# Block transposes of the mirrored squares one item behind their scores, and more room between the steps of the next batch's group norm

## The chip, the cores and the metric

The kernel runs on one core of one Trainium2 chip. The metric is device time in microseconds of one execution, the median over the runs shown; lower is better. The engines are TensorE (PE in the profile, with its weight loads as PEld), VectorE (DVE), ScalarE (ACT), GpSimd (POOL) and SyncE (SP), which only issues transfers here.

## The reference

The input x is float32 of shape (8, 128, 48, 48): 8 batches, 128 channels, 2304 positions. With C = 128 and n, m over positions:

```
# layer 0, for each batch
g   = group_norm(x, 32 groups)
x0  = concat(g, position embedding of 32 channels)
q,k,v = leaky_relu(W x0 + b)                    # each 128 x 2304
A   = softmax(q^T k / sqrt(128), masked to m <= n)
x   = x + v A^T                                 # causal attention
# layer 1, tokens t = x^T, 2304 x 128 a batch
h   = layer_norm(t)
t   = t + softmax(h h^T) h                      # full attention, no mask
u   = layer_norm(t) W^T, batch-normalized over all 8 x 2304 rows
y_s = sigmoid(u_s + y_{s-1} V^T)                # a recurrence over positions
out = t + y
```

Two facts of layer 1 matter. The score matrix h h^T is symmetric, so a block of exponentials (i, j) is the transpose of the block (j, i). And the group norm of batch b+1 depends on x alone, so it can be done while batch b is still in its attention.

## The kernel before

**Tiles.** Everything is float32. The 2304 positions of a batch are 18 blocks of 128 (NB), in 6 chunks of 384 columns (NQ = 6, QC = 384, QB = 3 blocks a chunk). One chunk of output stands in one PSUM bank and is summed over the 18 blocks of the other side.

**Two attentions as one stream of items.** For each batch, an object of `Causal` and one of `Full` list their items (method `items`). An item is one block m against one chunk j. `begin` issues its scores: a matmul into PSUM (line 1313 in `Full`), then ScalarE's exponential into a tile `p` in SBUF (line 1315). `product` issues the second matmul, which adds the item to the chunk's output `o` (line 1335), and does so three items later (LAG = 3 in the main loop, line 1518). A chunk's last product is followed by `after`, which copies `o` out and adds a chain of steps for the residual and the norm behind it. Batches follow each other in the one stream, so the next batch's projections and first scores mix with the end of the batch before.

**The symmetry in `Full`.** Chunk j computes scores only for blocks m >= 3j. There are three kinds of items:

- *direct*: scores and exponentials as above. Within the chunk's own 3 x 3 square of blocks, only the upper part is computed: own block g covers the columns from g x 128 on, so its matmuls have 384, 256 and 128 columns (`offset`). Own blocks 0 and 1 are begun first in a chunk.
- *turned*: for m < 3j the block was computed in chunk i < j, and is used transposed. VectorE transposes 32 x 32 squares when it was direct (`turned`, line 1280), SP stores the result as `e` (line 1229), and loads it back later as `g` (line 1221). Its product is line 1323.
- *mirrored*: the lower part of the chunk's own square, at the chunk's end (line 1331). It comes from `mirror`: two transposes on VectorE, `tm<-p` (line 1248), of 256 columns for own block 0 and 128 for own block 1. After the second, two transfers on GpSimd's queue follow: `m<-tm` (`out_of`, line 1261, to DRAM) and `gm<-m` (`back_in`, line 1265, four issues). The first must have landed before the second is issued. `mirror` is called from `product`, so three items behind the scores.

**Who decides the order.** The kernel writes its own order: within `manual_schedule` each engine executes instructions in the order in which Python emits them. Matmuls of the items form the backbone. Everything else (projections of the next batch, group norm, residuals, transfers) is a `Chain` of steps, and `Stream` keeps an account of time with which it places them: `now` is TensorE's, and `free` has one entry each for VectorE, ScalarE and GpSimd. A step is a triple: the work, its TensorE cost, and a list of (engine, us) that follows it. `Stream.then` books these on the engine's account, in turn; an entry with an empty name adds time without an engine, for a transfer or for room. A chain's next step is due at the time that `then` returns, and `tick`, called after each item, runs up to two steps that are due. So a number in such a list moves no work by itself: it moves the item after which the next step is emitted, and a booking made earlier also moves the due times of other chains.

**The group norm of the next batch.** `group_norm(b + 1)` is added as a chain when chunk 1 of `Full(b)` begins. `part1` has six `bn_stats` of 384 columns on VectorE and an aggregate (lines 805 and 807). `part2` averages over the groups with a tiny matmul, `gn_m` (line 813), and finishes with three small VectorE instructions. `part3` has a second tiny matmul, `gn_v` (line 824), one VectorE addition and the inverse square root on GpSimd (`gn_rs`, line 669). Its result is first read when the projection of the next batch starts, in chunk 4 (`begin`, j == NQ - 2).

**The residual behind a chunk of `Full`.** TensorE turns the output back (`of_t`, line 957), VectorE does the division, the residual, three pairs of statistics and a transpose (`dn` at line 1370 to `tt` at 1386), GpSimd a root (`roots`, line 1392), VectorE a small transpose of it (line 1397). SP stores root and row (`spread`, lines 1403 and 1406), loads them in another layout (`fetch`, lines 1410 and 1412), and TensorE multiplies by the weight (`wx`, line 1418), scaled on VectorE (1419) and copied by ScalarE (1424).

After the last batch, the recurrence runs over all batches at once (line 1660).

Of the kernel before, what the change touches and what calls it, by code (L numbers as in the profile page):

```python
# [604 lines left out]
def fast_path(ctx: ExitStack, tc: tile.TileContext, x, pe, w_ffn, out, x_tok, w_qkv, w_pos, v_t, gamma_beta, flag):  # L605
# [7 lines left out]
    QC = 384  # L613
    NQ = N // QC
    QB = QC // P
    SCALE = 1.0 / math.sqrt(P)
    US = 4 / 2400.0
# [46 lines left out]
    def rsqrt(pool, out_ap, var_ap, eps, tag):  # L664

        n = out_ap.shape[-1]
        ve = pool.tile([P, n], F32, tag=f"ve_{tag}", name=f"ve_{tag}")
        nc.vector.tensor_scalar_add(ve, var_ap, eps)
        nc.gpsimd.tensor_tensor(out_ap, ve, mhalf[:, :n], ALU.pow)

    with ExitStack() as actx:
# [16 lines left out]
        def psum_s(name):  # L688
            return ps_s.tile([P, CH], F32, tag="s", name=name)

        def psum_t(name):
            return ps_t.tile([P, CH], F32, tag="t", name=name)
# [97 lines left out]
        st = Stream()  # L790
# [7 lines left out]
        def group_norm(b):  # L798
            xt = xbuf[b]
            c = {}  # L800

            def part1():
                gs = small2.tile([P, NQ, 6], F32, tag="gn_st", name=f"gn_st_{b}")
                for j in range(NQ):
                    nc.vector.bn_stats(gs[:, j, :], xt[:, ts(j, QC)])  # L805
                mv = small2.tile([P, 2], F32, tag="gn_mv", name=f"gn_mv_{b}")
                nc.vector.bn_aggr(mv, gs)
                c["mv"] = mv

            def part2():  # L810
                mv = c["mv"]
                tp = psum_t(f"gn_m_{b}")
                nc.tensor.matmul(tp[:, 0:1], grp, mv[:, 0:1], start=True, stop=True)
                mg = small2.tile([P, 1], F32, tag="gn_mg", name=f"gn_mg_{b}")
                nc.vector.tensor_copy(mg, tp[:, 0:1])
                d = small.tile([P, 1], F32, tag="gn_d", name=f"gn_d_{b}")
                nc.vector.tensor_sub(d, mv[:, 0:1], mg)
                e = small2.tile([P, 1], F32, tag="gn_e", name=f"gn_e_{b}")
                nc.vector.scalar_tensor_tensor(e, d, d, mv[:, 1:2], ALU.mult, ALU.add)
                c["mg"], c["e"] = mg, e  # L820

            def part3():
                tp = psum_t(f"gn_v_{b}")
                nc.tensor.matmul(tp[:, 0:1], grp, c["e"], start=True, stop=True)
                rs = small2.tile([P, 1], F32, tag="gn_rs", name=f"gn_rs_{b}")
                rsqrt(small2, rs, tp[:, 0:1], 1e-5, "gn")
                norm_of[b] = c["mg"], rs

            return [(part1, 0.0, [("DVE", 3.6)]), (part2, 0.15, [("DVE", 0.6)]), (part3, 0.15, [("DVE", 0.15), ("POOL", 0.9)])]


        keys, vals, queries, largest, projected = {}, {}, {}, {}, {}
# [174 lines left out]
        class Causal:  # L1007


            def __init__(self, b):  # L1010
                self.b, self.sums, self.whose = b, {}, {}
# [14 lines left out]
            def begin(self, j, m, first):  # L1026
                b = self.b
                if first and b and j == 0:
                    st.advance(moved[b - 1], 2)
                if first:  # L1030
                    st.finish(projected[b, j])
                    allowed[b] = j + EARLY
                    following(b)
                    if j == NQ - 1:
                        bounds(b)
                off = self.offset(j, m)
                s = psum_s(f"s_{b}_{j}_{m}")
                nc.tensor.matmul(s[:, off:QC], keys[b][:, ts(m, P)], queries[b, j][:, off:], start=True, stop=True)  # L1038
                p = pp.tile([P, QC], F32, tag="p", name=f"p_{b}_{j}_{m}")
                nc.scalar.activation(p[:, off:], s[:, off:QC], AF.Exp, scale=SCALE)  # L1040
                ops = [("ACT", 0.16 + (QC - off) * 0.00085)]
                if m >= QB * j:
                    nc.gpsimd.tensor_mul(p[:, off : off + P], p[:, off : off + P], triu)  # L1043
                    ops.append(("POOL", 0.5))
                return p, st.then(st.spend((QC - off) * US), ops)
# [139 lines left out]
        class Full:  # L1185
# [6 lines left out]
            def __init__(self, b):  # L1192
                self.b = b
                self.tiles, self.stored, self.loaded = {}, {}, {}
                self.pairs = [(i, j) for j in range(NQ) for i in range(j)]
                self.used, self.to_store = 0, deque()

            @staticmethod
            def items():
# [88 lines left out]
            def begin(self, j, what, first):  # L1288
                b = self.b
                if j == 0:  # L1290
                    st.finish(normed_chunks[b, min(what[1] + 1, NB - 1) // QB])
                if first and b + 1 < B:
                    if j == 1:
                        norm_chain[b + 1] = st.add(group_norm(b + 1))
                    if j == NQ - 2:
                        st.finish(norm_chain[b + 1])
                        project(b + 1, 0)
                self.prefetch()
                if what[0] == "turned":
                    i, g = what[1:]  # L1300
                    while (i, j) not in self.loaded:
                        while self.pairs[len(self.loaded)] not in self.stored:
                            self.store()
                        self.load()
                    return self.loaded[i, j][:, :, g, :, :].rearrange("p a m r -> p m a r"), 0.0
                if what[0] == "mirrored":
                    st.finish(moved[b])
                    return self.gm.rearrange("p a q r -> p q a r"), 0.0
                m = what[1]
                off = self.offset(j, m)  # L1310
                xh = x_hat[b][1]
                s = psum_s(f"s1_{b}_{j}_{m}")
                nc.tensor.matmul(s[:, off:QC], xh[:, ts(m, P)], xh[:, j * QC + off : (j + 1) * QC], start=True, stop=True)  # L1313
                p = pp.tile([P, QC], F32, tag="p", name=f"p1_{b}_{j}_{m}")
                nc.scalar.activation(p[:, off:], s[:, off:QC], AF.Exp, bias=shift)  # L1315
                return p, st.then(st.spend((QC - off) * US), [("ACT", 0.17 + (QC - off) * 0.00085)])

            def product(self, j, what, o, p, ready, first, last):
                xhT = x_hat[self.b][0]
                if what[0] == "turned":  # L1320
                    i, g = what[1:]
                    out_ap = o[:, :QC].rearrange("p (m a r) -> p m a r", m=QB, a=R)
                    nc.tensor.matmul(out_ap, xhT[:, QB * i + g, :], p, start=first, stop=last)  # L1323
                    if g == QB - 1:
                        self.used += 1
                    cols = QC
                elif what[0] == "mirrored":
                    g = what[1]
                    cols = g * P
                    out_ap = o[:, :cols].rearrange("p (m a r) -> p m a r", m=g, a=R)  # L1330
                    nc.tensor.matmul(out_ap, xhT[:, QB * j + g, :], p[:, g - 1 : 2 * g - 1], start=first, stop=last)  # L1331
                else:
                    off = self.offset(j, what[1])
                    cols = QC - off
                    nc.tensor.matmul(o[:, off:QC], xhT[:, what[1], :], p[:, off:], start=first, stop=last)  # L1335
                    g = what[1] - QB * j
                    if g >= QB:
                        self.turned(j, what[1], p, ready)
                    elif g < QB - 1:
                        self.mirror(j, g, p, ready)  # L1340
                st.spend(cols * US, ready)

# [159 lines left out]
        for j in range(3):  # L1502
            positions(0, j)
        gn = st.add(group_norm(0))
        idle(psum_s("idle_m"), 2)
        st.advance(gn, 2)
# [23 lines left out]
        ready, o = {}, {}  # L1530
        for n in range(len(stream) + LAG):
            if n < len(stream):
                part, j, what, first, last = stream[n]
# [5 lines left out]
            if n >= LAG:  # L1539
                part, j, what, first, last = stream[n - LAG]  # L1540
# [16 lines left out]
    with ExitStack() as rctx:  # L1557
# [130 lines left out]
        off = rc.tile([P, 1], F32, tag="off", name="off")  # L1688
# [60 lines left out]
```

## Time and profile before

| | us |
|---|---|
| median of 3 runs | 1727.7 (1722.65, 1727.7, 1728.26) |
| the profiled execution | 1721.34 |
| its span in the profile | 1719.6 |
| TensorE busy | 1689.9 (98%) |
| VectorE busy | 1204.8 (70%) |
| ScalarE busy | 681.0 (40%) |
| GpSimd busy | 455.0 (26%) |
| mean granted TensorE clock | 0.996 |

The span is from the first to the last instruction that the profile holds; 1.7 us of the execution lie around it. The profile comes from one execution. The page gives busy time by engine, the chain of work that ended last (followed back from the end), groups of instructions with what ended the idle time before them, and transfers. Answers from the trace add the waits of one engine (who waited for whom, in total, how often, the longest) and a timeline. In these lines `p<-s` means a tile p written from a tile s; buffer and batch numbers are left out, so `gm<-m` stands for all batches and chunks. A float32 matmul shows as two passes, so a count of x2 is one matmul.

### The profile page before, as it was taken

The page shows a single profiled execution, that of the slowest core. Times are in us where ns is not written, and L with a number is a line of the kernel's source. Part 1 is how long each engine was busy: PE and PEld are TensorE (multiplying, and loading weights), DVE is VectorE, ACT ScalarE, POOL GpSimd, SP SyncE. Part 2 cuts the span into 40 slices and gives each one's busy share as a digit, 9 for nine tenths or more (in the row PEclk, how much of TensorE's full clock was granted, in tenths as well). Part 3 has the DMA queues.
Part 4 walks back from the last instruction along what each step waited for, and adds up shares of the span by engine and source line. Part 5 has one row for each costly group of instructions (what it writes and reads, how often), then busy time and mean ns, then how long its engine had stood idle before and what let it go on. Part 6 is the DMA issues. An engine that isn't in the chain of part 4 may idle for free.

```text
span 1719.6 us, 22539 instructions
## 1 busy us (share of the span) xinstructions
PE 1689.9 (98%) x6258; PEld 1084.3 (63%) x6259; DVE 1204.8 (70%) x3297; ACT 681.0 (40%) x1300; POOL 455.0 (26%) x637
## 2 busy tenths in 40 slices
PE   9999999999999999999999999999999999999996
PEld 5666666666666666666666666666666666666675
DVE  5875578656886478855687567865688657985467
ACT  3344324442344423434244333444234442344445
POOL 1222122411233222321224212332213312232115
PEclk9999999999999999999999999999999999999998
DMA  3347864568454884368644785457844587237867
GB/s 121 90 100 210 237 184 117 125 198 249 125 127 127 246 237 127 78 175 251 195 119 93 214 234 167 120 133 215 240 133 102 149 245 239 54 82 227 224 252 223
DMA packets 316732, 291.68 MB, mean 170 GB/s; under 512 B 195793, under 2 KB 280690, under 8 KB 315956
## 3 DMA queue, kind: packets, MB, share of 16 engines
q1 hardware_dynamic: 306572, 268.76, 54.9%
q0 software_dynamic: 9792, 20.99, 4.6%
q8 instruction: 52, 0.85, 0.2%
q14 instruction: 84, 0.69, 0.1%
q10 hardware_dynamic: 232, 0.40, 0.1%
HBM read 164.13 MB, written 125.90 MB: 169 GB/s over the span
## 4 chain that ended last, share of the span: by engine, by line
PE 88%; DMA 5%; DVE 4%; issue 1%; POOL 1%; SPq 1%; ACT 0%; DVEq 0%; POOLq 0%; ACTq 0%
PE s L1038 17%; PE o L1049 17%; PE s L1313 15%; PE o L1335 14%; PE o L1323 11%; PE pj L899 3%; DMA e<-t 2%; PE o L1331 2%; PE z L1660 2%; PE wx L1418 2%; PE pj L902 1%; DMA gm<-m 1%; DMA m<-tm 1%; PE of_t L957 1%; DVE gn_st L805 1%
## 5 line engine op out<-in xcount | busy, mean ns | idle before, releaser
L1315 ACT ACTIVATE p<-s,shift 128x384 f32<-128x384 f32 (+2 forms) x504 | 274.3, 550 | 562.7 <-PE s L1313 510.3
L1040 ACT ACTIVATE p<-s 128x384 f32<-128x384 f32 (+2 forms) x504 | 230.3, 460 | 399.7 <-PE s L1038 330.2
L1038 PE MATMUL s<-q,k 128*128 128x384 f32 (+2 forms) x1008 | 380.7, 459 | 0.0
L1313 PE MATMUL s<-xh 128*128 128x384 f32 (+2 forms) x1008 | 379.0, 458 | 0.0
L1049 PE MATMUL o<-p,vT 128*128 128x384 f32 (+2 forms) x1008 | 377.7, 456 | 0.0
L1335 PE MATMUL o<-p,xhT 128*128 128x384 f32 (+2 forms) x1008 | 367.8, 456 | 0.0
L1280 DVE STREAM_TRANSPOSE t<-p 128x384 f32<-128x384 f32 x360 | 183.4, 549 | 157.4 <-DMA e<-t 93.8
L1323 PE MATMUL o<-g,xhT 128*128 128x384 f32 x720 | 280.2, 486 | 0.0
L1335 PEld LDWEIGHTS o<-p,xhT 128*128 128x128 f32 x1008 | 189.6, 190 | 120.7 <-ACT p L1315 0.9
L1049 PEld LDWEIGHTS o<-p,vT 128*128 128x128 f32 x1008 | 186.7, 190 | 109.9 <-POOL p L1043 3.1
L1313 PEld LDWEIGHTS s<-xh 128*128 128x128 f32 x1008 | 183.6, 190 | 101.1
L1038 PEld LDWEIGHTS s<-q,k 128*128 128x128 f32 x1008 | 182.8, 190 | 98.5 <-issue 2.2
L1064 DVE TENSOR_TENSOR acc<-acc,p 128x384 f32<-128x384 f32 (+2 forms) x408 | 211.1, 517 | 24.2 <-DVE acc L1064 0.5
L1323 PEld LDWEIGHTS o<-g,xhT 128*128 128x128 f32 x720 | 131.8, 190 | 75.4 <-DMA g<-e 0.5
L1043 POOL TENSOR_TENSOR p<-p,triu 128x128 f32<-128x128 f32 x144 | 72.4, 505 | 343.5 <-ACT p L1040 343.3
L1265 POOL DMA_DIRECT2D gm<-m x192 | 107.0, 562 | 90.7 <-DMA m<-tm 50.4
L1392 POOL TENSOR_TENSOR roots<-ve_f,mhalf 128x3 f32<-128x3 f32 x48 | 41.9, 873 | 241.0 <-DVE ve_f L941 240.8
L947 POOL TENSOR_TENSOR rs_c<-ve_c,mhalf 128x3 f32<-128x3 f32 x48 | 48.3, 1006 | 173.3 <-DVE ve_c L941 173.2
L1138 POOL TENSOR_SCALAR xhT<-xhT 128x384 f32<-128x384 f32 x48 | 61.8, 1287 | 74.4 <-DVE yt L1150 39.1
L899 PE MATMUL pj<-xn,wT 128*128 128x384 f32 x192 | 79.3, 496 | 1.2 <-DVE xn L892 1.2
L1261 POOL DMA_DIRECT2D m<-tm x48 | 29.0, 603 | 189.7 <-DVE tm L1248 189.3
L1419 DVE TENSOR_TENSOR scale<-wx,scale 128x384 f32<-128x384 f32 x46 | 25.6, 557 | 74.0 <-PE wx L1418 66.4
(255 smaller groups left out, 1678.7 us busy)
## 6 DMA issues: line engine op xcount, KB each, us to landing
e<-t SPq DMA_DIRECT2D x480, 144.0 KB
g<-e SPq DMA_DIRECT2D x120, 576.0 KB
pb<-posb_d SPq DMA_DIRECT2D x42, 576.0 KB
t1t<-in_x_tok_dram SPq DMA_DIRECT2D x48, 192.0 KB
m<-tm POOLq DMA_DIRECT2D x48, 192.0 KB, 5.5
gm<-m POOLq DMA_DIRECT2D x192, 48.0 KB, 3.2
t_d<-tt SPq DMA_DIRECT2D x184, 48.0 KB
t2x<-t_d SPq DMA_DIRECT2D x46, 192.0 KB
```

Source lines behind the costliest of these rows:

```text
L899: nc.tensor.matmul(ps[:, :QC], wT[:, j, :], xn, start=True, stop=True)
L1038: nc.tensor.matmul(s[:, off:QC], keys[b][:, ts(m, P)], queries[b, j][:, off:], start=True, stop=True)
L1040: nc.scalar.activation(p[:, off:], s[:, off:QC], AF.Exp, scale=SCALE)
L1043: nc.gpsimd.tensor_mul(p[:, off : off + P], p[:, off : off + P], triu)
L1049: nc.tensor.matmul(o[:, off:QC], vals[b][:, ts(m, P)], p[:, off:], start=first, stop=last)
L1064: nc.vector.tensor_add(a[:, off:], a[:, off:], p[:, off:])
L1265: nc.gpsimd.dma_start(gm[ts(r, SQ)].rearrange("c a q r -> c a (q r)"), d.rearrange("(a c) b f -> b c a f", a=R)[r])
L1280: nc.vector.transpose(t[:, :, :, g, :].rearrange("p b j r -> p j b r"), p.rearrange("p (j b r) -> p j b r", j=QB, b=R))
L1313: nc.tensor.matmul(s[:, off:QC], xh[:, ts(m, P)], xh[:, j * QC + off : (j + 1) * QC], start=True, stop=True)
L1315: nc.scalar.activation(p[:, off:], s[:, off:QC], AF.Exp, bias=shift)
L1323: nc.tensor.matmul(out_ap, xhT[:, QB * i + g, :], p, start=first, stop=last)
L1335: nc.tensor.matmul(o[:, off:QC], xhT[:, what[1], :], p[:, off:], start=first, stop=last)
```

## The change

Two edits.

The first: in `Full`, for chunks j >= 1, `begin` puts the chunk's own blocks 0 and 1 into a queue `own` when their exponential has been issued, and the `begin` of the next item takes one entry from it and calls `mirror`. So VectorE's transpose is emitted one item behind the scores instead of three. For chunk 0 it stays in `product`. `mirror` itself, with its transposes and transfers, is as before.

The second: for b >= 1, the list of `part1` of the group norm gets an entry of 5.0 us without an engine, and that of `part2` one of 2.0 us. They are due times in the account; nothing is computed differently.

```diff
@@ group_norm
-            return [(part1, 0.0, [("DVE", 3.6)]), (part2, 0.15, [("DVE", 0.6)]), (part3, 0.15, [("DVE", 0.15), ("POOL", 0.9)])]
+            return [(part1, 0.0, [("DVE", 3.6), ("", 5.0 if b else 0.0)]), (part2, 0.15, [("DVE", 0.6), ("", 2.0 if b else 0.0)]), (part3, 0.15, [("DVE", 0.15), ("POOL", 0.9)])]
@@ Full.__init__
                 self.used, self.to_store = 0, deque()
+                self.own = deque()
@@ Full.begin
                         project(b + 1, 0)
+                if self.own:
+                    self.mirror(*self.own.popleft())
                 self.prefetch()
...
                 nc.scalar.activation(p[:, off:], s[:, off:QC], AF.Exp, bias=shift)
-                return p, st.then(st.spend((QC - off) * US), [("ACT", 0.17 + (QC - off) * 0.00085)])
+                ready = st.then(st.spend((QC - off) * US), [("ACT", 0.17 + (QC - off) * 0.00085)])
+                if j and 0 <= m - QB * j < QB - 1:
+                    self.own.append((j, m - QB * j, p, ready))
+                return p, ready
@@ Full.product
                     if g >= QB:
                         self.turned(j, what[1], p, ready)
-                    elif g < QB - 1:
+                    elif j == 0 and g < QB - 1:
                         self.mirror(j, g, p, ready)
```

## The prediction

> **What bounds the kernel now.** I read the page's first and fourth parts, then the list of waits of TensorE, then busy time by stage, then the timeline around one wait. First the page: busy shares, and the engines' shares of the chain that ended last.
>
> ```profile
> PE 1689.9 (98%) x6258; PEld 1084.3 (63%) x6259; DVE 1204.8 (70%) x3297; ACT 681.0 (40%) x1300; POOL 455.0 (26%) x637
> ...
> PE 88%; DMA 5%; DVE 4%; issue 1%; POOL 1%; SPq 1%; ACT 0%; DVEq 0%; POOLq 0%; ACTq 0%
> ```
>
> TensorE is the bound: only what it waits for, or executes more, can move the time. What it waits for (engine, line, releaser: total us, times, longest):
>
> ```profile
> PE o L1331 <- DMA gm<-m: 6.2, 5, 3.3
> PE gn_m L813 <- DVE gn_mv L807: 4.1, 6, 1.5
> ```
>
> These are the two waits that the diff aims at. The start and tail of the span hold the rest. By stage, TensorE's loss sits in the second attention (its eight stretches, then the first attention's seven; columns us, then busy time of PE, PEld, DVE, ACT, POOL):
>
> ```profile
> 726.00:830.00 104.00, 99.24 (x360) 62.26 (x358) 61.95 (x180) 39.95 (x69) 25.12 (x37) 1.00 0.74 210
> ...
> sum 818.00, PE 808.15 PEld 507.72 DVE 485.26 ACT 323.95 POOL 199.06; mean PE 101.02 PEld 63.47 DVE 60.66 ACT 40.49 POOL 24.88
> ```
> ```profile
> sum 711.00, PE 710.15 PEld 455.84 DVE 580.18 ACT 273.32 POOL 197.97; mean PE 101.45 PEld 65.12 DVE 82.88 ACT 39.05 POOL 28.28
> ```
>
> 9.9 us are idle in the second attention, 0.9 in the first. [...] I measured the waits by the distance between starts: a 384-column matmul pass is followed by the next after 0.323 us, and what exceeds that is a wait. Before `gm` it is 0.90, 0.69, 0.28, 3.47, 1.61, 0 and 0.34 us in batches 0 to 6, always chunk 4's `gm`: **7.29 us**. Before `gn_m` it is 0.79, 0.54, 1.62, 1.01, 0.35 and 0.13 in batches 1 to 6: **4.44 us**. No other wait over 0.12 us falls between 60 and 1640 us of the span.
>
> Why `gm` is late, in batch 1 (timeline; start, us):
>
> ```profile
> 402.57 0.47 ACT L1315 ACTIVATE p<-s,shift 128x256 f32<-128x256 f32 x1
> ...
> 404.51 0.44 DVE L1248 STREAM_TRANSPOSE tm<-p 128x256 f32<-128x256 f32 x1
> ...
> 405.89 0.55 DVE L1370 TENSOR_REDUCE dn<-of_t 128x3 f32<-128x384 f32 x1
> ...
> 409.68 0.27 DVE L1248 STREAM_TRANSPOSE tm<-p 128x128 f32<-128x128 f32 x1
> ...
> 410.25 0.61 POOL L1261 DMA_DIRECT2D m<-tm  x1
> ...
> 415.78 2.18 POOL L1265 DMA_DIRECT2D gm<-m  x4 [4.92 <-DMA m<-tm]
> ...
> 422.38 0.89 PE L1331 MATMUL o<-gm,xhT 128*128 128x128 f32 x4 [0.52 <-DMA gm<-m]
> ```
>
> The second block's exponentials end at 403.04, but its transpose runs at 409.68: VectorE does chunk 3's residual (`dn` to `tt`, 405.89 to 409.76) first. Then two transfers in series take 12.1 us to TensorE's use.
>
> [...] the transpose stood 6.6 us behind work that it doesn't need. [...] Here `m` takes 5.5 (median) from issue to landing and `gm` 3.2, so I use those. [...] So GpSimd stands 4.92 us before `gm`, as shown, and what follows `gm` on its queue waits too.
>
> **The change, part by part.** No instruction is added or removed but for splitting of matmul runs; 96 block transposes, 48 `m` and 192 `gm` issues remain. Everything is order, which the changed builder's own instruction lists show.
>
> *The mirrored squares.* In chunks 1, 2, 3 and 5 the two transposes keep their neighbours on VectorE (chunk 5's even precede a `scale` and `stats` pair). Only in chunk 4 do they move: ahead of `q`, `k`, `vT` and chunk 3's residual. The first then follows `xn` (ends 401.76), the second its exponentials (403.04), so it ends near 403.4 and `m` is issued near 403.7 instead of 410.25: 6.5 us earlier. With the same 12.1 us, `gm` is there at 415.8; TensorE wants it at 421.7 (422.38 less 0.69). In the worst batch, 3, `m` to use took 14.9 us (815.03 to 829.95, with a 2.37 us hole among the four issues); started 6.5 us earlier it ends at 823.4, wanted at 826.5. All six waits go: **-7.3 us**. What VectorE now does later: `q`, `k`, `vT` by up to 0.7 us, the residual by some 1.3, `xn` of the next piece from 410.90 to about 412.2; TensorE's projection using it stood at 414.14 and is placed one matmul later. Four PSUM score buffers cover the short hold of `pj`.
>
> *The group norm's room.* `gn_m` leaves its place before `of_t` and comes eight TensorE rows later, about 8 x 0.645 = 5.2 us, against a worst wait of 1.62; `gn_v` nine rows after that. Its VectorE steps sit after the transposes of block 9 and 12. `gn_rs` is needed by `xn` at 401, 45 us later. **-4.4 us**. The tiny matmuls cost the same pair of weight loads elsewhere; standing alone may cost 0.05 us more each, 14 x 0.05 = **+0.7**.
>
> *What the planner moves with them.* Earlier mirrors book VectorE and GpSimd earlier in its account, so GpSimd now issues chunk j's `gm` before the square root of chunk j-1's residual, and `m` before `gn_rs`. Root, its transpose, the spread and fetch on SP's queue and the `wx` matmul come later: `wx` by some 10 to 19 rows, its fetch by one or two other transfers. In chunk 3 of batch 1, `m` was issued at 385.53 and lands after 5.7; four issues of 0.55 and a root of 0.87 end at 394.3, and VectorE reaches the root's transpose, now after block 15 (393.93), at 394.5. In chunk 5: 423.44 + 7.1 + 2.2 + 0.9 = 433.6, reached about 434.8; with the slowest landing, 8.8, 435.3: half a us. Behind that wait stand transposes and sums whose readers have several us; zero, at most 1 us a batch if the cover went.
>
> *The last batch's end.* `wx` of chunk 3 now stands about three matmuls earlier than at 1641.43, near 1639.8, while its fetch has dropped behind `g_4_5` on SP (issued 1636.45, bound to chunk 4's last store). The row store before it ends near 1635.5; [...] the fetch is issued near 1638 and lands after 1640. I take **+1.0 us**, from 0 (if it lands in time) to 3 (behind 576 KB of `g_4_5` at some 300 GB/s, 1.9 us, with `scale` after it and an exponential on ScalarE behind `wx`).
>
> Sum: -7.3 - 4.4 + 0.7 + 1.0 = -10.0; half a us for small holds: **-9.5 us**. The profiled execution took 1721.34 (span 1719.6, 1.7 around it), so it would be 1711.8. The runs shown are 1722.65, 1728.26 and 1727.7: the profile lies below all. The `gm` wait already ranges from 0 to 3.47 by batch with transfer times, so I suppose, unproven, that the longer runs hold more of it. Taken off the median alone it gives 1718.2; I take the middle, **1715 us**.
>
> **Rivals.** *Half the gain stays out* (0.18, no measurable change, 1723 to 1732): `gm` is held by something other than the transpose, so that only `gn_m`'s 4.4 less 1 to 2 is won: about 1725. For it: batch 3's 2.37 us hole, which VectorE doesn't explain. Against: in batch 1 every step from transpose to landing follows without a gap over 0.8 us. *The change doesn't move the squares*: true for all chunks but the fourth, but none of these had a wait, so it only says where the gain is; it has no chance of its own.
>
> *A new wait on GpSimd makes it slower* (0.10, about 1737). Place: the root, behind `gm` and its wait for `m`, in chunks 2, 3 and 5; VectorE stands at the root's transpose, its block transposes stop, the six `p` buffers fill and TensorE starves. It decides where VectorE waits over some 4 us (VectorE's present stop of 4.73 before block 15's transposes in batch 1, for `e`'s store, starved TensorE only at `gn_m`), that is where `m` needs over 11 us; the longest now is 8.8. To lose, each of eight batches would have to pay 2.7 us: 8 x 2.7 = 21, less 11.7 won, 9 to 10 us slower. For it: the roots do move behind the transfers in all batches. Against: their readers were moved too.
>
> **How the numbers follow.** The likeliest case, both waits gone, has 0.72, and lies between 1707 and 1722. 0.3% of 1727.7 is 5.2 us, about what a measurement of this kernel tells from no change. So: faster 0.72, same 0.18, slower 0.10. The range reaches from 1707 (all of 11.7 and noisier runs' waits gone too) into the rival's half gain at 1729.
>
> **What would show it.** Right: TensorE's waits hold no chunk-4 `gm` and no `gn_m`; idle time in the seven middle second attentions falls from about 9 us to 1 or 2; both halves of `tm` in chunk 4 start within 2 us of each other; `m` follows `xn` by 2 to 3 us. The tail shows a wait before `wx` of 0 to 3 us. Wrong: a wait of TensorE on `s`, `p` or `wx` in every batch, VectorE idle over 4 us before the root's transpose, or `gm` still late with `m` issued early.

## The result, and the profile after

The changed kernel takes **1715.6 us** (median of 6 runs, 1714.85 to 1718.17), against 1724.84 (6 runs, 1721.73 to 1728.26) for the kernel before: a ratio of 0.9957, with a 95% interval of 0.9937 to 0.9976. The profiled execution took 1715.02, its span 1713.3, 6.3 us less than the 1719.6 of before. 1715 had been forecast. The two waits that the change aims at are gone, as the steps said; but part of what they gave, 5.8 us in this profile, was lost again in the last batch, where the forecast had set aside 1.0.

The page of the changed kernel first, with the busy line and the engines' shares of the chain that ended last.

```profile
PE 1687.8 (99%) x6259; PEld 1085.4 (63%) x6259; DVE 1209.1 (71%) x3297; ACT 684.8 (40%) x1300; POOL 449.9 (26%) x637
...
PE 96%; DMA 2%; DVE 1%; SPq 0%; issue 0%; ACT 0%; DVEq 0%; ACTq 0%
```

TensorE's share of the chain rose from 88 to 96%: followed back from the last instruction through the whole span, it is now almost nothing but TensorE's own work. Next, what TensorE waits for in the changed kernel (engine, line, releaser: total us, times, longest).

```profile
PE pw L1697 <- DVE off L1696: 6.8, 1, 6.8
PE wx L1424 <- DMA t2x<-t_d: 4.0, 1, 4.0
...
PE o L1329 <- DMA g<-e: 0.7, 2, 0.6
...
PE gn_m L813 <- DVE gn_mv L807: 0.5, 1, 0.5
```

No line for `gm` is left, and the one wait of `gn_m` is the first batch's, at the very start. New are two lines: 4.0 us once, before a `wx` in the last batch, and 0.7 us for two loads of `g`. The busy time by stage shows the first of them; the row is the last batch's second attention, the sum is over all eight (columns: us, then busy time of PE, PEld, DVE, ACT, POOL, the granted clock, the DMA share and GB/s).

```profile
1526.00:1642.00 116.00, 111.47 (x397) 69.86 (x396) 56.45 (x166) 45.20 (x77) 26.86 (x41) 0.99 0.69 201
sum 799.00, PE 794.47 PEld 502.56 DVE 469.10 ACT 307.82 POOL 192.77; mean PE 99.31 PEld 62.82 DVE 58.64 ACT 38.48 POOL 24.10
```

All 4.5 us that are left idle in eight second attentions are in the last batch; in the seven others TensorE is busy all the time by this measure. Last, the timeline around chunk 4 of batch 1, the place shown of the kernel before (start, us).

```profile
397.98 0.45 DVE L1249 STREAM_TRANSPOSE tm<-p 128x256 f32<-128x256 f32 x1 [2.28 <-ACT p L1318]
...
398.94 0.31 DVE L1249 STREAM_TRANSPOSE tm<-p 128x128 f32<-128x128 f32 x1 [0.52 <-ACT p L1318]
399.55 0.61 POOL L1262 DMA_DIRECT2D m<-tm  x1 [8.86 <-DVE tm L1249]
403.20 0.55 DVE L1376 TENSOR_REDUCE dn<-of_t 128x3 f32<-128x384 f32 x1
405.03 2.18 POOL L1266 DMA_DIRECT2D gm<-m  x4 [4.86 <-PE o L1329]
...
417.99 0.82 PE L1337 MATMUL o<-gm,xhT 128*128 128x128 f32 x4
```

Both transposes stand ahead of the residual (`dn`), and each waits for its exponentials and for nothing else. From the issue of `m` to TensorE's use there are now 18.4 us, where there were 12.1, and the matmul has no wait.

### The profile page after: what moved, and what is told of

It reads as the page before. It is cut to its first block, busy times and chain, and to the rows that moved or that the text cites. A ratio compares the mean times of both kernels' runs of the same rounds, so it can differ in the third digit from the quotient of the medians.

```text
span 1713.3 us, 22451 instructions
## 1 busy us (share of the span) xinstructions
PE 1687.8 (99%) x6259; PEld 1085.4 (63%) x6259; DVE 1209.1 (71%) x3297; ACT 684.8 (40%) x1300; POOL 449.9 (26%) x637
## 4 chain that ended last, share of the span: by engine, by line
PE 96%; DMA 2%; DVE 1%; SPq 0%; issue 0%; ACT 0%; DVEq 0%; ACTq 0%
PE s L1038 17%; PE s L1316 17%; PE o L1049 17%; PE o L1341 17%; PE o L1329 13%; PE pj L899 3%; PE pj L902 2%; PE o L1337 2%; PE z L1666 2%; PE wx L1424 2%; DMA g<-e 1%; PE of_t L957 1%; PE pb L847 0%; PE idle_last L1505 0%; DMA x<-in_x_dram 0%; DMA e<-t 0%
## 5 line engine op out<-in xcount | busy, mean ns | idle before, releaser
L1064 DVE TENSOR_TENSOR acc<-acc,p 128x384 f32<-128x384 f32 (+2 forms) x408 | 212.5, 521 | 23.1 <-DVE acc L1064 1.0
L1043 POOL TENSOR_TENSOR p<-p,triu 128x128 f32<-128x128 f32 x144 | 71.3, 497 | 356.1 <-ACT p L1040 355.8
L1138 POOL TENSOR_SCALAR xhT<-xhT 128x384 f32<-128x384 f32 x48 | 60.5, 1260 | 150.5 <-DVE yt L1150 121.2
L1249 DVE STREAM_TRANSPOSE tm<-p 128x256 f32<-128x256 f32 x96 | 33.9, 366 | 73.1 <-ACT p L1318 72.3
L906 DVE TENSOR_TENSOR q<-pj,pb 128x384 f32<-128x384 f32 x48 | 26.6, 554 | 50.1 <-PE pj L899 50.1
```

The lines of the kernel that those rows point to most:

```text
L1064: nc.vector.tensor_add(a[:, off:], a[:, off:], p[:, off:])
```

## The experiments

The first theory: each edit removed its own wait, and the early squares of the last batch cost the tail. Its rivals: one edit did all the work, or the tail is late for another reason. Each diff below is against the changed kernel. f2 means a second profile of the kernel before, whose start, unlike the first one's, holds no slow matmuls (passes that follow each other at twice their usual distance, 0.64 us for 384 columns where it is 0.32); spans are compared with its 1718.0. Waits are measured by the distance of starts, as in the prediction; the lists of waits count from the end of a busy mark, which for a pass of 384 columns is 0.49 us long where the next starts after 0.32, and come out somewhat smaller (in the first profile of the kernel before 6.2 us for `gm` and 4.1 for `gn_m`, against 7.29 and 4.44).

### The kernel before, and the changed kernel, once more

> The kernel before itself once more, for a second profile of it. Theory (the two waits are steady sums, though each batch's varies): chunk 4's gm waits 5 to 9 us in sum, gn_m waits 3.5 to 7 us, ratio 1.000 within 0.2%. Rival (the 7.3 us of gm in the first profile were a bad draw): gm waits under 4 us, which would explain why the early squares alone brought nothing that could be measured.

> The changed kernel itself once more, on this chip and beside these runs of the kernel before. Theory (its time is that of the first measurement): median 1714 to 1718, ratio 0.994 to 0.998, the wait before wx of chunk 3 in the last batch between 3 and 5 us and slow matmuls after it; no gm and no gn_m wait. Rival (the few first runs were lucky, since the squares alone and the kernel before range over 12 us): median over 1719, with slow matmuls in the first 25 us of the span.

The kernel before gave 1722.01 us (20 runs, 1716.78 to 1731.49), a ratio to itself of 0.9999 (0.9987 to 1.0011). The `gm` waits are 0.27, 3.06, 1.09 and 1.57 us, 5.99 in sum, and `gn_m`'s 0.57, 0.68, 1.20, 1.00, 0.39 and 1.23, 5.07 in sum; the first profile had 7.29 and 4.44. The sum of both is steadier (11.06 and 11.73) than its parts.

The changed kernel gave 1715.01 us (12 runs, 1712.36 to 1720.57), a ratio of 0.9954 (0.9941 to 0.9968). Its span is 1711.8, the tail's wait 3.2 us, and here no slow matmuls follow it. The effect is there again.

### The squares alone

```diff
-            return [(part1, 0.0, [("DVE", 3.6), ("", 5.0 if b else 0.0)]), (part2, 0.15, [("DVE", 0.6), ("", 2.0 if b else 0.0)]), (part3, ...
+            return [(part1, 0.0, [("DVE", 3.6)]), (part2, 0.15, [("DVE", 0.6)]), (part3, ...
```

> The change with the group norm's room taken out again; the squares stay early in all batches. Theory (each wait was removed by its own edit, and the 4.1 us wait before wx in the last batch, with the slower matmuls after it, belongs to the squares): no wait of chunk 4's gm, gn_m waits of about 4.4 us back in batches 1 to 6, the tail's 4.1 us wait still there; profiled span 1713.3 + 4.4 = about 1717.7. Rival (the early squares alone relieve VectorE before gn_m as well): gn_m waits under 1.5 us, span under 1715. Rival (the tail's wait came from the room): no wait before that wx, span about 1712.

Measured: 1724.55 us (22 runs), a ratio of 1.0005 (0.9992 to 1.0018): **no gain at all**. TensorE's waits in it:

```profile
PE gn_m L813 <- DVE gn_mv L807: 5.7, 6, 2.2
PE wx L1424 <- DMA t2x<-t_d: 3.1, 1, 3.1
```

The span is 1724.1, 6.1 more than f2's, and it adds up. No `gm` wait: -5.99. `gn_m`: 6.69 by distance of starts, +1.62. The tail: 3.24 of wait and 1.57 of slow matmuls after it, +4.81. The start: slow matmuls in the first 25 us, +5.81 (below). Sum: +6.25. Without the start it would be 0.4 above before: what the squares gain is taken by the tail and by `gn_m`. The theory holds for the kinds of waits, but not for independence: in this profile `gn_m` waits longer with the squares early, 6.69 us against 4.44 and 5.07 in the two profiles of the kernel before. What VectorE does before the longest of these waits, in batch 2:

```profile
550.11 1.50 DVE L1281 STREAM_TRANSPOSE t<-p 128x384 f32<-128x384 f32 x3 [6.45 <-DMA e<-t]
551.53 2.82 DVE L805 BATCH_NORM_STATS2 gn_st<-x 128x6 f32<-128x384 f32 x6
554.38 0.32 DVE L807 BATCH_NORM_AGGREGATE gn_mv<-gn_st 128x2 f32<-128x36 f32 x1
```

The group norm's statistics stand behind block transposes that wait 6.45 us for the store of `e` to free their buffer. In f2 the stop at this place is 4.63 us long, and the profile puts its end down to ScalarE's exponentials. Why the store ends later here was not tried.

### The room alone

```diff
-                if j and 0 <= m - QB * j < QB - 1:
+                if False and 0 <= m - QB * j < QB - 1:
...
-                    elif j == 0 and g < QB - 1:
+                    elif True and g < QB - 1:
```

> The change with the squares put back where the kernel before has them; only the group norm's room stays. Theory: no gn_m wait, chunk 4's gm waits stay at some 7 us over the seven batches (each between 0 and 4), no wait before wx in the last batch; profiled span 1719.6 - 4.4 + 0.2 = about 1715.4. Rival (the group norm's VectorE work, now later, runs into the squares or gives them room): gm waits over 10 us or under 4 us, span over 1718 or under 1712.

Measured: 1713.83 us (6 runs), ratio 0.9952 (0.9939 to 0.9965); the profiled span is 1715.3, as the theory said. TensorE's `gm` waits are all there:

```profile
PE o L1337 <- DMA gm<-m: 6.5, 3, 2.9
```

Against f2: -5.07 for `gn_m`, +0.97 for `gm`, +1.5 for slow matmuls after the longest `gm` wait, -2.6 in sum, and the spans differ by -2.7. The median gained more than that, partly by luck: the mean granted clock of the six runs is 0.9955, that of the 27 runs of before beside them 0.9939, a difference of 0.0016, worth an estimated 0.0016 x 1720 = 2.8 us. So by the medians the room alone does as much as the whole change (0.9952 against 0.9957 and 0.9954). The profiled spans, 1715.3 against 1713.3 and 1711.8, are no measure of this, since the profiled run is the slowest of the six. That pointed to the tail.

### The last batch as before

> The change, but in the last batch the squares stand where the kernel before has them. Theory (in the last batch the early squares only pull TensorE's wx of chunk 3 ahead of its fetch: 4.1 us of wait, and after it some 1.7 us lost to matmuls at half the pace): neither is there, profiled span 1713.3 - 5.8 = about 1707.5. Rival (the fetch is late because the whole kernel runs ahead of its transfers, whatever the squares do in the last batch): a wait of 3 us or more before a wx in the last batch stays, span over 1711. Rival (the slower matmuls come by themselves): wait gone, some 1.7 us of slow matmuls left, span about 1709.2.

That kernel did something else than its text says: the condition in `product` read the `b` of the main loop, which is the last batch by then, so in chunks 1 to 5 of batches 0 to 6 the squares were transposed and moved **twice** (35 more `m`, 140 more `gm` issues). It took 1799.95 us (6 runs), a ratio of 1.0427 (1.0397 to 1.0458), so its numbers say nothing on the tail; they say what a busier GpSimd does (VectorE has 70 transposes more, too). TensorE's waits:

```profile
PE o L1049 <- POOL p L1043: 26.5, 7, 5.7
PE o L1337 <- DMA gm<-m: 23.6, 7, 4.3
```

The first line is in no list of the prediction: the causal mask of the *next* batch's first attention (L1043, on GpSimd) stands behind the second attention's transfers. A kernel meant to leave only chunk 4 out had the same slip (chunks 1, 2, 3 and 5 twice, chunk 4 once and late):

> As the run with the last batch as before, but chunk 4's squares too stand where the kernel before has them in every batch; chunks 1, 2, 3 and 5 keep the change. Theory (only chunk 4's squares move on VectorE past other work, so all of the gain in gm waits is there): gm waits of chunk 4 some 7 us as in the kernel before, no gn_m wait, span about 1707.5 + 7.3 = 1714.8. Rival (the reordering of GpSimd's queue in the other chunks brings part of it): gm waits under 4 us, span under 1712.

It took 1791.31 us, ratio 1.0416 (1.0384 to 1.0448), and its question was put again further down. The last batch with each square made once:

```diff
-                if j and 0 <= m - QB * j < QB - 1:
+                if j and b < B - 1 and 0 <= m - QB * j < QB - 1:
...
-                    elif j == 0 and g < QB - 1:
+                    elif (j == 0 or self.b == B - 1) and g < QB - 1:
```

> The change, but in the last batch, and only there, the squares stand where the kernel before has them; each square is made once (the earlier kernel of this aim made all of them twice). Theory (in the last batch the early squares only pull TensorE's wx of chunk 3 ahead of its fetch: 4.1 us of wait, and after it some 1.7 us lost to matmuls at half the pace): neither is there, span about 1713.3 - 5.8 = 1707.5 if the start is like the changed kernel's. Rival (the fetch is late because the whole kernel runs ahead of its transfers): a wait of 3 us or more before a wx in the last batch stays, span over 1711. Rival (the slow matmuls come by themselves): wait gone, some 1.7 us of slow matmuls left, span about 1709.2.

This kernel, f3 from here on, took **1710.02 us** (6 runs, 1708.75 to 1711.14), a ratio of 0.9927 (0.9913 to 0.9942). The slowest of these runs is faster than the fastest of the changed kernel beside them (1712.36). The span is 1707.6, as the theory had it. The whole list of TensorE's waits over 0.3 us:

```profile
PE pw L1697 <- DVE off L1696: 7.4, 1, 7.4
PE idle L1505 <- POOL ident masks.py:199: 1.7, 1, 1.7
PE pj L899 <- DVE xn L892: 1.5, 2, 0.9
PE of_t L957 <- ACT of L1361: 0.9, 1, 0.9
PE wx L1464 <- ACT xc L1460: 0.6, 1, 0.6
PE gn_m L813 <- DVE gn_mv L807: 0.5, 1, 0.5
PE pb L847 <- DMA pe<-position_rows: 0.4, 1, 0.4
```

All of these stand in the kernel before as well, in the first 60 us or in the end, but for the last, 0.4 us at the start. So the early squares of the last batch were what made `wx` wait, and the slow matmuls went with the wait. In the changed kernel this is what TensorE does there:

```profile
1627.04 0.49 PE L965 MATMUL tk<-ident,t 128*128 128x128 f32 x3
1631.49 0.88 PE L1424 MATMUL wx<-t2x,w1T 128*128 128x384 f32 x2 [3.96 <-DMA t2x<-t_d]
1632.21 0.92 PE L1329 MATMUL o<-g,xhT 128*128 128x384 f32 x2
1632.91 0.64 PE L1316 MATMUL s<-xh 128*128 128x128 f32 x2
1633.34 3.52 PE L1329 MATMUL o<-g,xhT 128*128 128x384 f32 x6
```

and this what SP issues:

```profile
1624.72 0.81 SPq L1222 DMA_DIRECT2D g<-e  x2
1625.96 0.32 SPq L1416 DMA_DIRECT2D t2x<-t_d  x1
```

The fetch `t2x` goes out at 1625.96, behind two loads of `g` of 576 KB each, and by the last of the completions that the trace records for it, it lands at 1631.35, 5.4 us later; TensorE is at `wx` at 1627.4, 1.4 us after the issue. In the kernel before, SP and TensorE did this:

```profile
1631.52 1.23 SPq L1221 DMA_DIRECT2D g<-e  x2
1632.84 0.40 SPq L1410 DMA_DIRECT2D t2x<-t_d  x1
...
1641.43 0.81 PE L1418 MATMUL wx<-t2x,w1T 128*128 128x384 f32 x2
```

There the fetch also stood behind two loads, and it took even longer to land, 7.7 us. Nothing waited, because `wx` came 8.6 us after the issue. In f3 it is the same: issued at 1619.44, landed after 6.8 us, wanted after 8.9 (1628.31). So what the early squares changed is not how long the fetch takes, but its lead, the time from its issue to its use. Measured against the same matmul of scores (at 1624.09 before, at 1611.64 in the changed kernel, 12.45 us earlier), the fetch goes out 5.6 us later and `wx` comes 1.6 us earlier: of a lead of 8.6 us, 1.4 are left.

### Matmuls in the place of the wait

```diff
                 def product():
...
+                    if b == B - 1 and j == NQ - 3:
+                        idle(psum_s("idle_wx"), 40)
                     tp = psum_t(f"wx_{b}_{j}")
```

> The changed kernel with 40 more matmuls of the identity, whose result nobody reads, ahead of wx of chunk 3 in the last batch: 40 x 0.107 = 4.3 us of TensorE work in the place of the 4.1 us wait. Theory (the half-paced matmuls after the wait come from TensorE having stood still): no wait over 1 us there, the matmuls after it 0.32 us apart, span about 1713.3 + 0.2 - 1.7 = 1711.8. Rival (the slow spell has another cause, for instance memory traffic of the transfers): the matmuls after it are 0.64 us apart as before, span about 1713.5.

A float32 matmul shows as two passes, so the 40 are 80 records and take 8.6 us, not 4.3; the forecast of the span forgot that. The span is 1722.7, with a slow start like that of the squares alone (below).

```profile
1634.20 9.10 PE L1507 MATMUL idle_wx<-ident 128*128 128x128 f32 x80
1643.13 0.81 PE L1426 MATMUL wx<-t2x,w1T 128*128 128x384 f32 x2
...
1644.64 2.10 PE L1329 MATMUL o<-g,xhT 128*128 128x384 f32 x6
```

There is no wait before `wx`, and the six matmuls of the last line take 2.10 us where they took 3.52. So the slow matmuls went with TensorE's standing still. The transfers as their cause are not excluded by this run alone, since it moves the matmuls 4.5 us away from them. The second profile of the changed kernel does that: there the same transfers stand in the same place, and no slow matmuls follow, after a wait of 3.2 us where the first had 4.1 (why not was not shown). The time is 1718.6 us (20 runs), ratio 0.9974 (0.9961 to 0.9987): worse than the change, since 8.6 us stand in the place of 4.1 + 1.7.

### Chunk 4 alone, and all but chunk 4

Conditions as in the last diff of the last batch, with `j == NQ - 2` for `j` in the first and its opposite in the second kernel.

> The group norm's room, and early squares in chunk 4 alone, in all batches but the last; chunks 1, 2, 3 and 5 have theirs where the kernel before has them. Theory (on VectorE only chunk 4's squares pass other work, so only they bring anything): no gm and no gn_m wait, span within 1 us of 1707.6, the kernel with the last batch as before; ratio about 0.993. Rival (the early squares of the other chunks and the new order on GpSimd's queue carry part of it): waits of gm in chunk 4 of over 2 us in sum, span over 1709.5.

> The complement: the room, and early squares in chunks 1, 2, 3 and 5 but not in chunk 4, in all batches but the last (each made once). Theory: chunk 4's gm waits are back with 5 to 8 us in sum, no gn_m wait, span about 1707.6 + 6 to 7.5 = 1713.6 to 1715, ratio about 0.996. Rival: gm waits under 2 us, span under 1710.

Chunk 4 alone: 1708.93 us (6 runs, 1707.79 to 1714.3), ratio 0.9916 (0.9897 to 0.9934), span 1705.2, no `gm` wait and no `gn_m` wait behind the start. It is the fastest kernel of this study, though its interval overlaps f3's. All but chunk 4: 1739.96 us, ratio **1.0083** (1.0066 to 1.0100), span 1740.1, so the theory is right that chunk 4 holds the gain and wrong on what is left without it: not 7 us worse than f3, but 32. TensorE's waits there:

```profile
PE o L1337 <- DMA gm<-m: 14.6, 7, 2.7
PE o L1329 <- DMA g<-e: 6.8, 3, 2.7
```

`gm` of chunk 4 is late in all seven batches, by 1.9 to 2.8 us; three loads of `g` are late by 2.1 to 2.8, and half of these ten waits are followed by slow matmuls. The waits are 23.1 us in sum, the five slow stretches an estimated 8.5 (five times the 1.7 us in the tail of the changed kernel). So the early squares of the other chunks are no harmless company. A likely reason is that they book VectorE and GpSimd earlier in the kernel's own account and so push the steps of other chains about; no run separates this from other reasons.

### GpSimd held: where the rival would decide

Both holds are added to the kernel with the last batch as before.

```diff
                 def back_in():
+                    nc.gpsimd.memset(gm, 1.0)
+                    for _ in range(10):
+                        nc.gpsimd.tensor_scalar_mul(gm, gm, 1.0)
```

> The kernel with the last batch as before, and in every chunk GpSimd works for 10 x 1.26 + 0.3 = about 13 us (it fills and scales gm's own tile, which the transfer then overwrites) between the issue of m and that of gm, as if m took 13 us to land. By the prediction's rival, whose bound was 11 us: VectorE stands over 4 us at the root's transpose in chunks 2, 3 and 5, TensorE starves on s or p of the second attention by 2 to 3 us a batch, 14 to 21 us in all, span 1722 to 1729. By the place that the kernel with doubled squares showed: the first causal mask of the next batch, which stood 6 us behind gm of chunk 5 on GpSimd's queue, comes some 5 us late, TensorE waits at the product L1049 by 2 to 5 us in each of seven batches and loses 1 to 3 us more to slow matmuls after each: 20 to 50 us, span 1728 to 1758, and no wait in the second attention but chunk 4's gm. Third case (both are covered): span under 1711.

Measured: 1930.56 us (2 runs), ratio 1.1192. The hold was larger than planned, because filling `gm` also waits for the tile's last reader (2.71 us at 462.88 us of the span), and it held chunk 0, where GpSimd's scaling of the normalized rows (`xhT`, L1138) came late for TensorE: 66.9 us of waits, beside 75.4 for `gm` itself. The place was not settled; so a cleaner one:

```diff
                 def back_in():
+                    if j in (2, 3, 5) and b < B - 1:
+                        for _ in range(8):
+                            nc.gpsimd.tensor_scalar_mul(tm..., tm..., 1.0)
```

> A cleaner hold than the last one, whose filling of gm's tile also waited for that tile's last reader, and which held chunks 0 and 4 too. The kernel with the last batch as before; in chunks 2, 3 and 5 of the other batches GpSimd, once m has landed, multiplies m's source by one 8 times (8 x 1.26 = 10 us) before it issues gm: as if m took 15 us instead of 5, beyond the 11 us that the prediction's rival gave as its bound. By that rival: VectorE stands at the root's transpose over 4 us in each of these chunks, its block transposes stop and TensorE starves on s or p in the second attention by 2 to 3 us a batch, span 1722 to 1729. By the mask: in chunk 5 the causal mask at L1043 stands behind gm and the root and has 0.7 us to spare before TensorE's L1049 (430.81 + 0.45 against 431.92 in batch 1), so it comes some 4 us late in each of seven batches, with 1 to 3 us of slow matmuls after it: 7 x 5 to 7 = 35 to 49, span 1743 to 1757, with TensorE's waits named L1049 on p of L1043 and nothing over 1 us in chunks 2 and 3. Third case (covered): under 1712.

Measured: 1775.97 us (2 runs), ratio 1.0313 (1.0191 to 1.0436), span 1769.0, above what either side gave. TensorE's longest waits:

```profile
PE o L1049 <- POOL p L1043: 25.3, 7, 5.5
PE o L1340 <- DMA gm<-m: 12.9, 11, 1.8
```

and VectorE's:

```profile
DVE roots_t L1406 <- POOL roots L1401: 113.7, 21, 8.3
```

VectorE stood at the root's transpose 21 times, 5.4 us on average and up to 8.3, and TensorE waited for nothing on `s` or `p` in the second attention. What it paid there is the hold itself: the held `gm` of chunks 2 and 3 came up to 1.9 us late. Four loads of `g` were late as well, 5.3 us in sum where the kernel without the hold has 0.2; whether through VectorE's stops was not traced. The larger price is the mask: seven waits of 2.7 to 5.7 us, 26.5 in sum by distance of starts, and slow matmuls after six of them.

### What the runs show beside the kernels: slow starts

The kernel before ranges from 1717.25 to 1736.78 us in 47 runs, the longer ones with a lower mean granted clock (0.997 down to 0.990). Of the nine profiles of kernels that are no slower than it, three lost clock in the first 25 us: the first of the kernel before, the squares alone, and the busy tail. The same stretch of the kernel with the squares alone

```profile
10.00:23.00 13.00, 13.00 (x36) 8.41 (x36) 5.83 (x14) 1.93 (x4) 0.71 (x2) 0.52 0.19 76
```

and of the changed kernel

```profile
10.00:23.00 13.00, 12.34 (x57) 7.66 (x57) 8.60 (x20) 3.48 (x8) 1.94 (x4) 1.00 0.21 84
```

has a granted clock (the number after POOL's) of 0.52 against 1.00, for the same instructions: 36 matmul records instead of 57 in 13 us. The first `pj` that waits, at 56.2 us, is at 62.0 there. The profile of the kernel before that the prediction used had lost 1.6 us in this way (clock 0.83 from 10 to 20 us). Of the longest runs, 1731 to 1737 us, there is no trace, so where they lost their time is not shown. In the runs with a mean clock of 0.997 the changed kernel took 1712.5 to 1713.9 us and the one with chunk 4 alone 1707.8 to 1708.6.

## Why the prediction was right, and where not

**The `gm` wait, -7.3.** Right in kind and cause: the transposes, done before the residual, let `m` go 6.3 us earlier in relation to its use (6.5 forecast), and no `gm` wait is left. Chunk 4 alone brings it, as the step said. The size is 6 to 7.3, since the wait itself varies between profiles (5.99 in f2). Two details were off: `m` follows `xn` by 3.9 us and not 2 to 3, because VectorE waits 2.28 for the exponentials; and batch 3 still has a 2.4 us hole among its four `gm` issues, which now costs nothing.

**`gn_m`, -4.4.** Right: gone in batches 1 to 6, in the change and with the room alone (4.4 to 5.1).

**Tiny matmuls, +0.7, and small holds, +0.5.** Neither is there. `gn_m` follows the matmul before it after 0.32 us as in a row of matmuls. From the first `pj` that waits to the tail's `of_t`, f3 is 10.58 us shorter than f2, whose waits there were 11.06, and f3 has one new wait of 0.33: 0.15 us are left for all such costs, where 1.2 were forecast; the 0.05 us for each tiny matmul had no measurement under it.

**The last batch's end, +1.0 (0 to 3).** This is the term of the sum that was mis-sized; it was 5.8. The place was named rightly: the fetch of `wx`, issued later on SP, while `wx` comes earlier. Both were even timed rightly: the fetch near 1638 and `wx` near 1639.8 are 1625.6 and 1627.35 in the changed kernel, less the 12.45 us gained before them, and they stood at 1625.96 and 1627.4. What failed is the time from the fetch's issue to its landing. With a wait of 1.0 the step has it land some 3 us after the issue, the author's estimate without a measured landing of such a fetch; it took 5.4, so that the wait was 4.1 and lay outside the 0 to 3. The trace that the prediction was made from had a longer one, 7.7 us for this same fetch, hidden under the 8.6 us that it had then. And nothing in the step foresaw that matmuls can run at half the pace after such a wait, 1.7 us more. f3 shows the whole term by taking it away.

**The sum.** In the profiled executions: waits gone -7.3 and -4.4; the start's slow matmuls of the kernel before, not there after, -1.6; the tail +5.8; two new waits for `g` (batches 2 and 3) +1.1. That makes -6.4, and the spans differ by -6.3; -9.5 was forecast. That the forecast of 1715 met 1715.6 is luck in part. The sum gave 1711.8 for the profiled execution, which took 1715.02; the forecast then took the middle between this sum and the median, because the runs of before are longer than their profile. The reason that it gave for that, more `gm` wait in the longer runs, is not shown. What the traces show is slow matmuls at the start of some, and over the 27 runs of before the time goes with the clock (correlation -0.81).

**The rivals.** *Half the gain stays out* was the size of what the tail takes, but not its mechanism: `gm` was held by nothing else. *A new wait on GpSimd* did not occur: VectorE waited at the root 1.5 us in the whole kernel (three times). Its place and bound fell by the second hold on GpSimd: VectorE may stand 5 us and more at the root without a wait of TensorE on `s` or `p`; the place that decides is the causal mask L1043 behind `gm` and the root of chunk 5, with 0.7 us to spare in the change (batch 1, 430.81 + 0.45 against 431.92). The prediction did not list it, though it was the nearest cliff.

## What to carry to other kernels

Follow an early transfer to the end of the loop: in the last iteration nothing refills the pipeline, and work that comes earlier can meet a fetch that does not (here a wait of 4.1 us, and 1.7 us of slow matmuls after it). Move only the instance that has a wait (chunk 4 here, and not in the last batch: 0.9916 against 0.9954 for all), because in a kernel whose order comes from an account of time each early booking can move other chains, as the kernel with all but chunk 4 suggests. And test two edits apart: here the room alone gave all of the measured gain, and the squares added to it only once their tail was mended (0.9927 against 0.9952, whose intervals just touch; with chunk 4 alone, 0.9916, they are apart). Before you call a transfer covered, read how long it takes to land in the trace of before, where its lead may have hidden it (7.7 us here).

## What the runs showed of the hardware

In these traces a wait of TensorE can cost more than its length: the 4.1 us before `wx` in the changed kernel were followed by 1.7 us of slow matmuls. Counted over the 14 traces, between 100 us and the tail's last matmuls: waits (excess of the distance between two starts) over 1 us, and how many were followed within 8 us by three or more passes at twice their usual distance.

| wait, us | waits | followed by slow matmuls |
|---|---|---|
| 1 to 2 | 39 | 2 |
| 2 to 2.5 | 15 | 7 |
| 2.5 to 3 | 11 | 7 |
| 3 to 3.5 | 17 | 10 |
| over 3.5 | 33 | 32 |

In this count the slow passes mostly begin 0.4 to 1.5 us after TensorE resumes, and end some 3 to 5.5 us after it; they cost 1.5 us in the median (0.7 to 2.4). The record of the granted clock holds them as well. Here are two neighbouring stretches in the tail of the changed kernel, in its first profile and in its second (the clock is again the number after POOL's):

```profile
1629.37:1632.78 3.41, 1.29 (x4) 0.87 (x5) 0.32 (x1) 1.14 (x1) 0.00 (x0) 1.00 0.61 178
1632.78:1636.19 3.41, 3.41 (x8) 2.06 (x7) 1.56 (x5) 1.88 (x3) 0.00 (x0) 0.50 0.29 115
```
```profile
1625.83:1629.24 3.41, 1.98 (x9) 1.03 (x7) 0.26 (x1) 0.83 (x1) 2.40 (x5) 1.00 0.96 363
1629.24:1632.65 3.41, 1.80 (x7) 1.28 (x8) 0.75 (x2) 1.33 (x2) 0.00 (x0) 1.00 0.47 125
```

In the first, TensorE resumes with `wx` at 1631.49, and from 1632.78 to 1636.19 the granted clock is 0.50. In the second, the wait of 3.2 us lies within the two stretches shown, and the clock is 1.00 in both. Other profiles show the same two outcomes. With the squares alone, after 3.24 us of wait before `wx`, the clock is 0.76 from 1640 to 1644 us and 0.81 from 1644 to 1648; with the room alone, around its longest `gm` wait of 2.9 us, it is 0.88 from 820 to 824 and 0.69 from 824 to 828. In the first profile of the kernel before, around and after the 3.47 us before `gm` in batch 3, it is 1.00 from 824 to 836. So in these traces the length of a wait from 2 to 3.5 us does not say whether slow matmuls follow (24 of the 43 in the table), and what decides it was not shown.

The first 25 us are not covered by the count. There the clock is 0.50 from 12.63 to 16.04 us in the first profile of the kernel before, and from 12 to 24 us with the squares alone; the cause stays open. The slow matmuls in this part cost 0 to 5.8 us, nearly as much as the 6.3 us by which the change shortened the profiled span.
